# The rows of an image's chunks in DRAM: 64 KB apart, or 72 KB with an unused ninth chunk

## The chip, the core and the metric

The kernel runs on one core of a Trainium2 chip. The core has a matrix engine (TensorE, in profiles PE, its weight loads PEld), three engines for elementwise work (VectorE or DVE, ScalarE or ACT, GpSimd or POOL), and SyncE (SP), which here issues most of the DMA transfers. Sixteen DMA engines move data between the core's own memory (SBUF, 128 partitions) and DRAM. Matrix products land in PSUM, a small memory of its own. The metric is the time of one execution on the device in microseconds (us), the median of several runs.

## The reference, cut to what matters

Sixty-four images of 256 x 256 go through a Fourier neural operator of four layers with 32 channels; its output, joined to 77 rows of text, goes through one transformer layer (attention and a feed-forward part that works on selected rows). All is float32.

```
v = concat(x, gx, gy) @ p_w + p_b                    # 64 images, 32 channels, 256 x 256
for i in range(4):
    x_ft = rfft2(v);  keep 24 x 12 modes;  mix channels with W1, W2;  x1 = irfft2(...)
    x2 = einsum('bcxy,cd->bdxy', v, w_w[i]) + w_b[i]
    v = batch_norm(x1 + x2)                          # mean and variance over all images
    if i < 3: v = relu(v)
h = einsum('bcxy,cu->bxyu', v, q_w) + q_b            # 64 x 256 x 256
h = concat(h, txt);  h = h + attention(layernorm(h));  h = h + ffn(layernorm(h))
```

A field `v` of one image has 32 x 256 x 256 numbers, 8.4 MB. The 64 of them, 537 MB, don't fit into SBUF, so that each layer reads them from DRAM and writes them back.

## The kernel before, in words

**The tensors in DRAM.** `vd` at line 183 is a list of 2 x 64 DRAM tensors, two for each image, that are used in turn: layer 0 writes the first set, layer 1 reads it and writes the second, layer 2 reads the second and writes the first, and the transformer reads the first. Each is `[128, 8, 8, S]` with `S` = 256, float32: 128 rows, one for each SBUF partition; 8 chunks; 8 image rows of 256 numbers in each chunk. A chunk's part of one row is 8 x 256 x 4 B = 8 KB, so that the rows are 8 x 8 KB = 64 KB apart.

**The stages.** `forward_first` reads the input and makes the modes for layer 0 without storing a field. For each layer `mix` then multiplies the modes by their weights and finds the batch norm's factors, and `layer(i, ...)` (line 549) for i = 0, 1, 2 makes the field of all images. After layer 3's `mix` there is no field to be stored: `image_rows` (line 970) reads the stored field of layer 2 directly and projects it to one channel, and `attention`, `select` and `feed_forward` follow.

**A layer.** It goes image by image and chunk by chunk (`b`, `t`). `ld` (line 655, in layers 1 and 2 only) loads one chunk into a tile `vin` with two transfers of 0.5 MB, of four image rows each, issued at line 661. `pre` (line 681) adds up in PSUM the inverse transform (the products at line 687) and, in layers 1 and 2, the channel mixing of the loaded chunk (line 698). `ev` (line 705) evicts the sum through the ReLU into a tile `vo`, half by ScalarE or VectorE at line 710 or 712, as the order says. `st_` (line 716) stores `vo` with two transfers of 0.5 MB, issued at line 719. `turn` (line 721) transposes it; `prod` and `sq` (lines 729 and 741) take the next layer's squares for its batch norm; `y`, `half`, `zt`, `x_`, `xo` and `xs` make the field's modes and store them (lines 750 to 808). `am` loads and scales the mixed modes of a later image (lines 624 to 638), and in layer 0 `lx` loads rows of the input (line 640).

There are four buffers of `vin` in layers 1 and 2 and four of `vo` in all three layers, so that an eviction needs a `vo` tile whose store has landed, and a load needs a `vin` tile that TensorE has read. PSUM is one ring of four tiles, taken in order of release.

**What sets the order.** The layers are written under a manual schedule: `ORDER` (line 128) holds one string of steps for layer 0 and one for layers 1 and 2, and the loop at line 834 runs them in that order for each image, with `@1` for a step of the image after and `@-1` for one of the image before. Every load, store and mode transfer of a layer, apart from the input rows, is issued on SP's queue in this order. In layers 1 and 2 the loads of an image stand among the stores of the image before:

```
"pre5 sqB7@-1 zt1@-1 sqA7@-1 pre6 evA5.a ld2@1 st4 evB5.d st5 turn4 evA6.a prod5 x@-1 "
"evB6.a sqB5 prod6 sqA5 xo@-1 turn5 pre2@1 sqA6 turn6 sqB6 prod4 evA2.a@1 evB2.d@1 "
"sqB4 ld0@1 ld7 sqA4 pre0@1 evB0.d@1 ld3@1 prod2@1 st6 evA0.a@1 turn2@1 sqB2@1 sqA2@1 "
```

**The transformer.** `image_rows` loads a whole chunk `ch` with one transfer of 1 MB (line 990), where each partition's part is 8 KB in one piece, in a pool of seven buffers, and TensorE reads it at line 992. It runs two images ahead.

The instructions that touch `vd` are the store at line 719, the load at line 661 and the load at line 990. All three index a chunk by its number (0 to 7).

Of the kernel before, what the change touches and what calls it, by code (L numbers as in the profile page):

```python
# [9 lines left out]
F32 = mybir.dt.float32  # L10
# [6 lines left out]
S = 256  # L17
# [136 lines left out]
def tile_fno_fusion_transformer(ctx: ExitStack, tc: tile.TileContext, a, cst_d, grid_d, out):  # L154
    nc = tc.nc
    x = a["x"].rearrange("b x y o -> b x (y o)")
    B = x.shape[0]
# [4 lines left out]
    dram = ctx.enter_context(tc.tile_pool(name="dram", bufs=1, space=DRAM))  # L162
# [17 lines left out]
    epsc = const.tile([128, 1], F32, name="epsc")  # L180
    nc.vector.memset(epsc, EPS)

    vd = [dram.tile([128, 8, 8, S], F32, name=f"v{b}_{n}") for n in range(2) for b in range(B)]
    vd = [vd[:B], vd[B:]]
    mix_d = [dram.tile([2, M, 2, B, 32 * C], F32, name=f"mix{i}") for i in range(L)]
    xh_d = [dram.tile([128, B, 144], F32, name=f"xh{i}") for i in range(1, L)]
# [1057 lines left out]
```

## Time and profile before

| What | Value |
|---|---|
| Time, median of 3 runs | 11,274.06 us (11,268.07 to 11,280.38) |
| The profiled execution's own time | 11,266.44 us |
| Its span in the trace | 11,264.7 us |
| Granted TensorE clock, mean | 0.984 |
| Layer 0, first store to last mode store issued | 193 to 2555 us |
| Layer 1, first load to last mode store issued | 2610 to 5562 us |
| Layer 2, likewise | 5620 to 8560 us |
| DMA packets, bytes | 971,776, 3457.30 MB |
| Read from DRAM, written to it | 1733.60 MB, 1696.92 MB |

How to read what follows. The page's first part gives the busy time of each engine with its share of the span; a busy TensorE is not a TensorE at its peak, since its products are pipelined. The row of q1 is SP's DMA queue: packets, MB, and the time its packets took as a share of sixteen engines over the stretch asked for. A row of a transfer has the tile written, the tile read, the queue, how many, KB each, and the median time in us from issue to landing. A row of a stretch has its ends and length in us, the busy us of each engine with the number of instructions, then TensorE's granted clock, the mean busy share of the DMA engines, and GB/s. A row of a wait names the engine and line that waited, what it waited for, us in all, times, and the longest. The chain is the work that ended last, followed back from the end step by step; its shares are of the stretch asked for.

### The profile page before, as it was taken

Reading aid. Unit: us, or ns where it says so; the run is one execution under the profiler, and the core shown is the slowest. Engines: PE = TensorE matmul, PEld = TensorE weight load, DVE = VectorE, ACT = ScalarE, POOL = GpSimd, SP = SyncE. Lnnn points to the kernel's source line nnn. Section 1 sums busy time; section 2 is a strip of 40 time slices with the busy share of each in tenths; the row PEclk is TensorE's granted clock in tenths of the full one; section 3 lists DMA queues with packets and bytes.
Section 4 is the critical chain, followed back from the end, with each engine's and each line's share of the span. In section 5 each row is a group of like instructions: output and inputs, shape, how many; then the busy total and the mean of one; then the engine's idle time right before and its main releaser. Section 6 shows DMA issues by size and latency. Waiting matters only on the chain.

```text
span 11264.7 us, 409247 instructions
## 1 busy us (share of the span) xinstructions
PE 10600.1 (94%) x182550; PEld 5728.7 (51%) x182550; DVE 8446.4 (75%) x10381; ACT 6475.0 (57%) x10673; POOL 1448.0 (13%) x2179
## 2 busy tenths in 40 slices
PE   6999999998999999999799999999996999999999
PEld 3555555554444444444444444444443666666666
DVE  6888888887777777777677777777776666666665
ACT  5777777775656555566556566556664333333333
POOL 1111111110000000000000000000000333333333
PEclk8999999998999999999999999999998999999999
DMA  6776676678999999999899999999998555555553
GB/s 214 248 248 246 246 249 246 246 252 322 381 383 384 378 379 375 376 379 379 316 366 386 379 376 381 382 380 378 375 379 301 224 228 228 225 226 227 225 227 137
DMA packets 971776, 3457.30 MB, mean 307 GB/s; under 512 B 149016, under 2 KB 198552, under 8 KB 903064
## 3 DMA queue, kind: packets, MB, share of 16 engines
q1 hardware_dynamic: 904576, 3366.80, 77.7%
q0 software_dynamic: 58288, 60.60, 2.3%
q8 instruction: 1429, 23.41, 0.8%
q10 hardware_dynamic: 7144, 3.72, 0.1%
q14 instruction: 339, 2.78, 0.1%
HBM read 1733.60 MB, written 1696.92 MB: 305 GB/s over the span
## 4 chain that ended last, share of the span: by engine, by line
PE 61%; DMA 21%; DVE 9%; ACT 4%; issue 3%; SPq 2%; POOL 0%; ACTq 0%; DVEq 0%; POOLq 0%
PE ring L757 15%; DMA v<-vo 11%; PE ring L687 9%; PE ring L735 8%; DMA vin<-v 6%; PE ring L698 5%; PE hp L992 4%; PE ring L667 3%; PE pp L1155 3%; PE pp L1166 3%; PE ring L791 2%; PE pp L1120 2%; DVE vo L712 2%; PE pp L1185 2%; DMA xh<-xo 2%
## 5 line engine op out<-in xcount | busy, mean ns | idle before, releaser
L746 ACT ACTIVATE ring<-ring 128x1024 f32<-128x1024 f32 x3072 | 3115.9, 1014 | 1176.6 <-PE ring L735 1114.9
L724 DVE STREAM_TRANSPOSE t<-vo 128x2048 f32<-128x2048 f32 x1536 | 3465.4, 2286 | 21.1 <-DVE vo L712 0.9
L735 PE MATMUL ring<-vo,w 32*32 32x512 f32 x49152 | 2401.5, 599 | 80.3 <-ACT vo L710 64.2
L712 DVE TENSOR_SCALAR vo<-ring 128x1024 f32<-128x1024 f32 x1280 | 1543.8, 1221 | 1191.4 <-PE ring L698 805.3
L710 ACT ACTIVATE vo<-ring 128x1024 f32<-128x1024 f32 x1792 | 1792.2, 1023 | 1039.9 <-PE ring L698 498.1
L757 PE MATMUL ring<-t,cst 32*32 32x512 f32 x49152 | 2063.5, 599 | 46.4 <-issue 40.2
L757 PEld LDWEIGHTS ring<-t,cst 32*32 32x32 f32 x49152 | 909.6, 103 | 917.1 <-issue 615.9
L735 PEld LDWEIGHTS ring<-vo,w 32*32 32x32 f32 x49152 | 801.3, 103 | 1064.7 <-issue 397.6
L687 PE MATMUL ring<-cst,y 24*128 24x256 f32 x16384 | 1232.6, 403 | 76.8 <-DVE vo L712 59.5
L634 POOL TENSOR_TENSOR ams<-ams,bns 48x512 f32<-48x512 f32 x384 | 401.1, 1045 | 6964.8 <-DMA ams<-mix 6692.2
L698 PE MATMUL ring<-vin,ws 32*32 32x512 f32 x32768 | 1278.0, 603 | 17.9 <-issue 14.0
L687 PEld LDWEIGHTS ring<-cst,y 24*128 24x128 f32 x16384 | 789.8, 185 | 992.8 <-DVE vo L712 389.1
L675 DVE STREAM_TRANSPOSE y<-ring 128x1024 f32<-128x1024 f32 x384 | 762.7, 1986 | 320.0 <-PE ring L667 319.0
L687 PE MATMUL ring<-mv,y 29*128 29x256 f32 x8192 | 705.1, 403 | 36.6 <-ACT ring L746 20.2
L687 PEld LDWEIGHTS ring<-mv,y 29*128 29x128 f32 x8192 | 455.9, 185 | 370.2 <-ACT ring L746 209.8
L791 PEld LDWEIGHTS ring<-cst,zt 128*128 128x128 f32 x4608 | 533.6, 193 | 176.7 <-ACT vo L710 113.8
L767 ACT COPY half<-ring 128x1024 f32<-128x1024 f32 x192 | 194.5, 1013 | 723.9 <-PE ring L757 723.9
L1193 POOL DMA_DIRECT2D out_dram<-o x1024 | 511.2, 508 | 664.8 <-DVE o L1188 622.9
L746 ACT ACTIVATION_READ_ACCUMULATOR ring<-ring 128x1 f32 x3072 | 585.4, 191 | 0.0
L791 PE MATMUL ring<-cst,zt 128*128 128x96 f32 x4608 | 565.6, 280 | 6.2 <-DVE zt L775 6.0
L775 DVE STREAM_TRANSPOSE zt<-ring 128x1024 f32<-128x1024 f32 x192 | 377.4, 1965 | 242.8 <-PE ring L757 242.8
L667 PE MATMUL ring<-ams,cst 49*128 49x512 f32 (+1 forms) x1536 | 450.4, 641 | 108.7 <-POOL ams L634 40.1
(374 smaller groups left out, 9759.8 us busy)
## 6 DMA issues: line engine op xcount, KB each, us to landing
v<-vo SPq DMA_DIRECT2D x3072, 512.0 KB, 7.9
vin<-v SPq DMA_DIRECT2D x2048, 512.0 KB, 9.0
ch<-v SPq DMA_DIRECT2D x512, 1024.0 KB, 13.9
mix<-ob SPq DMA_DIRECT2D x48, 1024.0 KB, 5.3
ams<-mix SPq DMA_DIRECT2D x384, 96.0 KB, 8.0
xin<-in_x_dram SPq DMA_DIRECT2D x16, 1024.0 KB, 8.2
mv<-in_x_dram POOLq DMA_DIRECT2D x256, 64.0 KB, 7.2
out_dram<-o POOLq DMA_DIRECT2D x1024, 16.0 KB, 3.1
```

Of the source, the lines that this page charges most:

```text
L667: nc.tensor.matmul(ps[:, n, :], lhsT=EX[hv, 128 * h:128 * h + 128], rhs=ams[b % 2][hv], start=True, stop=True, skip_group_check=True,)
L675: nc.vector.transpose(y_[b, h].rearrange("p q c -> p c q"), ring[key][0][1].rearrange("p n (c k) -> p (n c) k", k=32),)
L687: nc.tensor.matmul(ps[n][:, 256 * r:256 * r + 256], lhsT=y_[b, t // 4][32 * n:32 * n + K, q:q + 4, :].rearrange("p q c -> p (q c)"), rhs=m ...
L698: nc.tensor.matmul(ps[n][32 * j:32 * j + 32], lhsT=ws[32 * n:32 * n + 32], rhs=v[32 * n:32 * n + 32, 2 * j:2 * j + 2, :], start=False, sto ...
L710: nc.scalar.activation(to, ring[key][h][1], AF.Relu)
L712: nc.vector.tensor_scalar(to, ring[key][h][1], 0.0, None, ALU.max)
L724: nc.vector.transpose(t32[b, t // 2][:, :, 8 * (t % 2):8 * (t % 2) + 8, :].rearrange("p y s c -> p s y c"), vo[b, t].rearrange("p s (y l) ...
L735: nc.tensor.matmul(ps[n][32 * j:32 * j + 32], lhsT=w4[i + 1][32 * n:32 * n + 32], rhs=vo[b, t][32 * n:32 * n + 32, 2 * j:2 * j + 2, :], st ...
L746: nc.scalar.activation(ps, ps, AF.Square, accum_out=acc[:, at:at + 1])
L757: nc.tensor.matmul(ps[n][32 * j:32 * j + 32], lhsT=FYT[32 * n:32 * n + 32, k, :], rhs=t32[b, j][32 * n:32 * n + 32, k].rearrange("p s c -> ...
L791: nc.tensor.matmul(ps[:, 0, 96 * g:96 * g + 96], lhsT=zt_[:, h, k0:k0 + 4, :].rearrange("p k c -> p (k c)"), rhs=FX[:, h, 48 * r:48 * r + ...
L1193: nc.gpsimd.dma_start(out[b, 64 * n + 16 * g:64 * n + 16 * g + 16].rearrange("(p t) d -> p t d", t=2), o[32 * g + 8 * n:32 * g + 8 * n + 8 ...
```

## The change

The DRAM tensors of the fields have nine chunks in place of eight. The loops and the transfers go over chunks 0 to 7 as they did; the ninth is neither written nor read. Rows are 9 x 8 KB = 72 KB apart.

```diff
-    vd = [dram.tile([128, 8, 8, S], F32, name=f"v{b}_{n}") for n in range(2) for b in range(B)]
+    vd = [dram.tile([128, 9, 8, S], F32, name=f"v{b}_{n}") for n in range(2) for b in range(B)]
     vd = [vd[:B], vd[B:]]
```

## The prediction

> **What bounds the kernel now.** I read the page's top, to see how near the engines and the DMA are to full; then stretches of each stage side by side; then the DMA answer for the stages that touch the padded tensors; then waits and chain there.
>
> ```profile
> span 11264.7 us, 409247 instructions
> PE 10600.1 (94%) x182550; PEld 5728.7 (51%) x182550; DVE 8446.4 (75%) x10381; ACT 6475.0 (57%) x10673; POOL 1448.0 (13%) x2179
> q1 hardware_dynamic: 904576, 3366.80, 77.7%
> v<-vo SPq DMA_DIRECT2D x3072, 512.0 KB, 7.9
> vin<-v SPq DMA_DIRECT2D x2048, 512.0 KB, 9.0
> ch<-v SPq DMA_DIRECT2D x512, 1024.0 KB, 13.9
> ```
>
> The three kinds of transfer that the diff touches are 3072 stores and 2048 loads of 0.5 MB and 512 loads of 1 MB: 5120 x 0.524 + 512 x 1.049 = 3221 MB of the 3367 MB on SP's queue. So nearly all of the kernel's DMA traffic changes address, and nothing else changes.
>
> ```profile
> core 0: us, PE busy (x) PEld busy (x) DVE busy (x) ACT busy (x) POOL busy (x), PEclk, DMA share, GB/s
> 1000.00:1500.00 500.00, 485.48 (x9234) 253.98 (x9248) 442.38 (x247) 378.74 (x599) 60.41 (x84) 1.00 0.69 246
> 3000.00:3500.00 500.00, 479.77 (x10350) 227.11 (x10334) 380.21 (x212) 302.51 (x478) 25.10 (x24) 1.00 0.99 382
> 7500.00:8000.00 500.00, 479.57 (x10279) 228.29 (x10277) 376.61 (x211) 301.41 (x477) 23.01 (x22) 1.00 0.99 379
> 9500.00:10500.00 1000.00, 974.77 (x5954) 678.04 (x5953) 673.69 (x2418) 379.70 (x773) 331.50 (x575) 1.00 0.57 225
> ```
>
> These are layer 0 (stores only), layers 1 and 2 (loads and stores), and the transformer (loads only). In layer 0 and in the transformer the DMA engines are busy 69% and 57% of the time while TensorE is busy 97%: there the padded tensors are not the limit. In layers 1 and 2 TensorE has 96%, but the DMA share is 99%. This is where an address can cost or save time. The first and last instruction of each layer put them at 2610 to 5562 us and 5620 to 8560 us, 5892 us together, 46 us an image.
>
> ```profile
> by line: DMA v<-vo 21.0%; PE ring L757 19.0%; DMA vin<-v 12.4%; PE ring L698 10.3%; PE ring L687 9.5%; PE ring L735 7.5%; PE ring L667 4.7%; DVE vo L712 2.8%; issue 2.6%; SPq L661 2.5%; PE ring L791 2.3%; ACT vo L710 2.3%; DMA ams<-mix 1.9%
> ```
>
> ```profile
> ACT vo L710 <- DMA v<-vo: 52.4, 36, 3.3
> DVE vo L712 <- DMA v<-vo: 48.2, 35, 3.3
> PEld ring L698 <- DMA vin<-v: 4.9, 9, 1.1
> ```
>
> Both are of 4000 to 5000 us, in layer 1. About 35% of the chain is DMA (21.0 + 12.4 + 1.9), and the evictions at L710 and L712 wait some 100 us in 1000 for a store to release one of the four `vo` buffers. So a change of the store's or load's speed is felt between two ends: by 35% of it (the chain's share), and by all of it (the DMA share of 0.99).
>
> **The change, part by part.** *Instructions.* None is added, removed or moved. A store at L719 still moves, for each partition, four rows of 256 numbers that lie one after the other: 4 x 256 x 4 B = 4 KB; a load at L990 still 8 KB. So packets stay as many and as large: 0 us. No wait and no queue order changes. *The ninth chunk.* Loops run over eight; 128 x 8 KB = 1 MB an image is never written or read: 0 us. *Addresses.* The 128 rows of one transfer stood 64 KB apart, so that they agreed in the low 16 bits; now they stand 72 KB apart and take eight different positions in a 64 KB frame. This is the only term, and its price is to be read from how long packets take now.
>
> ```profile
> q1 hardware_dynamic: 107162, 374.38, 97.1%
> v<-vo SPq DMA_DIRECT2D x352, 512.0 KB, 9.1
> vin<-v SPq DMA_DIRECT2D x352, 512.0 KB, 9.2
> ```
>
> (The DMA answer for 4000 to 5000 us.) The two kinds make 704 x 128 = 90,112 packets of 4 KB in these 1000 us. The packet records behind this answer give their durations over both layers: 87% take 159 to 161 ns, the mean is 168 ns. 4096 B in 159 ns is 25.8 GB/s, and sixteen engines at that rate make 412 GB/s. Loads and stores both run at this floor, in layer 1 and in layer 2, where the source and the destination tensors change places. In the transformer, 8 KB reads have their own floor of 309 ns (26.5 GB/s) with a mean of 319. A floor that seven packets in eight reach is the DMA engine's own pace, not a memory bank waited for. If rows 64 KB apart fought over the same part of the memory, most packets would be stretched, and the ones of stores and loads differently.
>
> What is left to win is the tail: 168 - 159 = 9 ns a packet. Each 0.5 MB transfer has 8 packets on each of 16 engines; layers 1 and 2 have 2048 stores and 2048 loads. So 1 ns of mean packet time is 4096 x 8 ns = 32.8 us of DMA time, and the whole tail is 9 x 32.8 = 295 us. Is the tail aliasing? I sorted the packets by start into groups of 128. Most groups of either layer have an excess of 0 to 6 ns a packet; the excess sits in three or four groups an image with 20 to 65 ns, at the same place in the order of work (around the loads of chunks 7, 3 and 1, a run of six to eight transfers issued close together where the queue has been worked off and starts anew). (The grouping is rough, by a few us.) In image 0, whose loads are issued in another order, three of the four groups of chunks 3 and 1 have 0 ns. In layer 0, where stores alone use the tensor, the tail too goes by place in the order (54 and 68 ns at the two stores of chunk 3, 6 ns at those of chunks 1 and 2), and by image it is level. A tail that follows the order and not the address is not removed by a new pitch. I take 0 of it, and keep both ends: -295 us if all of it were aliasing and all were felt, and on the other side a new pattern that stretches packets.
>
> For that side the nearest row is layer 0's own packets: mean 176 ns, a 17 ns tail, at a share of 0.69. If the new addresses brought the tail of layers 1 and 2 to that, it would be 8 x 32.8 = 262 us of DMA time, of which 35% to all is felt: +92 to +262 us. In layer 0 and the transformer the same 8 ns is covered by TensorE: the DMA share of 0.69 would go to 0.72. With this cover gone (packets more than 40% longer) those stages would turn DMA-bound as well; nothing here points to that.
>
> **Two rules of the Trainium skill weighed.** The page "DMA: Bandwidth & Descriptors", section "Latency and other measured facts", has a row on HBM row pitch at large powers of two: copies of 128 rows reach 207 GB/s in each direction at a pitch of 512 KiB and 164 at 2 MiB, against 214 with a pad, and it advises a pad of a few KiB. This speaks for a gain. The loss shrinks with the pitch, and the page has no figure for 64 KB; if its smallest loss, 1 - 207/214 = 3.3%, held here, the 168 x 32.8 = 5505 us of packet time would shrink by 180 us at most, an estimate from that page, and the kernel would take some 11,090 us. The packets at their floor here say that the loss is nearer to none. The same page, section "Where 436 GB/s comes from", holds that transfers between HBM and the core are bound by the memory's side, at about 358 GB/s. Were that so, the order of addresses would be what sets the time in layers 1 and 2. The trace has 377 to 382 GB/s in these layers, above that limit, with each engine at a fixed pace; the measurement decides. By the rule the term lies anywhere in -295 to +262; by the row it is 0.
>
> **The sum.** 0 for instructions, 0 for the ninth chunk, 0 for the addresses: the profiled execution of 11,266 us (11,264.7 of span and 2 around it) stays. It lies 8 us under the median of the three runs shown, 11,274, and inside their spread of 11,268 to 11,280. I predict **11,272 us**.
>
> **The rivals.** *Faster, aliasing is real.* For it: the DMA share of 0.99, the tail of 9 ns, the skill's row. Against it: the floor, and the tail's place. Half of the tail gone and felt by half: 295/4 = 74 us, 11,200 us; all of it, 10,980, less what TensorE's 96% takes back: with 4% of idle time in 5892 us it can shorten these layers by 236 us at most, so 11,040. *Slower, the new pitch maps worse.* Rows with equal low bits may be spread evenly by the memory's address map just because they are a power of two apart, and 72 KB may pile several of the sixteen engines on one bank. The place is the same saturated queue of layers 1 and 2, whose late stores hold the `vo` buffers, so L710 and L712 evict later, the ring of PSUM tiles frees later and TensorE's next product starts later. The price is 32.8 us for each ns that is felt; with layer 0's tail and the chain's share of 35% that is +92, or 11,365 us, and with all of it felt 11,535. It decides from 22.5 us, which is 0.7 ns a packet if all is felt and 2 ns at 35%. For it: that point is low, and no run shows this pitch. Against it: no packet kind shows a dependence on address. *The change does nothing at the memory*[...]: that is my forecast.
>
> **How the numbers follow.** A measurement of this kernel tells about 0.2% (22.5 us) from no change. I give the forecast 0.55, faster 0.22, slower 0.23. The sensitivity of 33 us for each ns is why the forecast has no more: a shift of 0.5% in packet time would be seen. The forecast's own range is 11,250 to 11,295. For eight in ten, each rival keeps about one in ten outside: of the gains I cut those over 110 us, of the losses those over 90: 11,160 to 11,360.
>
> **What would show it.** Right: packet floor of 159 ns, mean within 1 ns of 168, 379 to 383 GB/s and a DMA share of 0.98 to 0.99 in the stretches of layers 1 and 2, landings of 9.1 and 9.2 us, 46 us an image, the same chain. Faster: over 390 GB/s there, landings under 9 us, TensorE busy over 97%, and fewer waits of L710 and L712 for stores. Slower: the DMA share stays at 0.99 with under 375 GB/s, landings above 9.5 us, and those waits grow past 100 us in 1000. I would be wrong most simply if the tail is the memory's after all, or if a mapping that looked free at 64 KB is not at 72.

## The result, and the profile after

The changed kernel takes 11,234.72 us in the median of 6 runs (11,230.22 to 11,240.62), the kernel before 11,273.67 us beside it. The ratio is 0.9965, with a 95% interval of 0.9952 to 0.9977: **faster by 0.35%**, some 39 us. The profiled execution after has a span of 11,229.3 us, 35.4 us under the one of before.

The page of the changed kernel, its top and its transfers, in the order shown of before:

```profile
span 11229.3 us, 409247 instructions
PE 10577.1 (94%) x182550; PEld 5734.1 (51%) x182550; DVE 8449.2 (75%) x10381; ACT 6476.7 (58%) x10673; POOL 1447.8 (13%) x2179
q1 hardware_dynamic: 904576, 3366.80, 77.7%
v<-vo SPq DMA_DIRECT2D x3072, 512.0 KB, 7.9
vin<-v SPq DMA_DIRECT2D x2048, 512.0 KB, 9.0
ch<-v SPq DMA_DIRECT2D x512, 1024.0 KB, 12.9
```

Instructions, packets and bytes are the same to the last one, and the share of q1 too: the same transfers in 0.3% less time. Of the transfer rows only the landing of `ch` moved (13.9 to 12.9 us), in the transformer, whose time is as before. Where the time went is seen from where each layer begins and ends (first load or store issued to last mode store issued):

| | before | after | difference |
|---|---|---|---|
| layer 0 | 2346 us | 2343 us | -3 |
| layer 1 | 2952 us | 2930 us | -22 |
| layer 2 | 2941 us | 2929 us | -12 |
| from layer 2's end on | 2715 us | 2715 us | 0 |
| mean 4 KB packet, layers 1 and 2 | 168.2 ns | 167.4 ns | -0.8 |
| mean 4 KB packet, layer 0 | 176.4 ns | 176.6 ns | +0.2 |
| mean 8 KB packet, transformer | 320.6 ns | 320.2 ns | -0.4 |

The lengths are of the trace's own times. The beginnings and ends given with the profile of before lie some 11 us late against the views (there layer 1 runs from 2599 to 5551 us), and layer 0's 193 us should be 209 on that count.

So 34 of the 35 us come from the two layers that load and store, and next to none from the stages that only store or only load. Stretches long enough to smooth the images' beat, of the kernel before:

```profile
core 0: us, PE busy (x) PEld busy (x) DVE busy (x) ACT busy (x) POOL busy (x), PEclk, DMA share, GB/s
1000.00:2400.00 1400.00, 1361.39 (x25865) 713.39 (x25870) 1244.25 (x692) 1064.96 (x1686) 166.92 (x232) 1.00 0.70 247
3000.00:5000.00 2000.00, 1917.85 (x40975) 906.22 (x40961) 1504.11 (x839) 1203.32 (x1896) 94.14 (x90) 1.00 0.98 379
6000.00:8000.00 2000.00, 1917.05 (x41031) 908.99 (x41017) 1506.43 (x842) 1207.77 (x1903) 92.04 (x88) 1.00 0.98 380
9000.00:11000.00 2000.00, 1952.88 (x11922) 1361.23 (x11918) 1349.31 (x4837) 760.62 (x1550) 658.33 (x1145) 1.00 0.58 226
```

and of the changed kernel:

```profile
1000.00:2400.00 1400.00, 1362.60 (x25940) 716.13 (x25936) 1246.46 (x693) 1068.15 (x1692) 167.78 (x233) 1.00 0.70 247
3000.00:5000.00 2000.00, 1924.22 (x41234) 915.67 (x41236) 1515.96 (x845) 1211.46 (x1907) 92.06 (x88) 1.00 0.98 381
6000.00:8000.00 2000.00, 1921.28 (x41184) 917.05 (x41167) 1511.74 (x843) 1215.51 (x1915) 92.03 (x88) 1.00 0.98 381
9000.00:11000.00 2000.00, 1951.51 (x11926) 1358.88 (x11926) 1349.08 (x4844) 760.14 (x1549) 658.55 (x1145) 1.00 0.58 226
```

In layer 1 (the second row of each) the DMA share stays at 0.98 while 381 GB/s move in place of 379, and VectorE gets 845 instructions done in place of 839; layer 2 (the third row) goes from 380 to 381. Layer 0 and the transformer keep 247 and 226 GB/s. TensorE's granted clock is 1.00 in every row, so that it isn't the cause. The waits and the chain of layer 1, 4000 to 5000 us as before:

```profile
ACT vo L710 <- DMA v<-vo: 45.2, 38, 2.6
DVE vo L712 <- DMA v<-vo: 43.8, 37, 2.5
```

```profile
by line: DMA v<-vo 22.7%; PE ring L757 18.9%; DMA vin<-v 13.7%; PE ring L698 9.1%; PE ring L687 8.5%; PE ring L735 7.0%; PE ring L667 4.7%; SPq L661 3.1%; issue 2.6%; ACT vo L710 2.5%; DVE vo L712 2.5%; PE ring L791 2.0%; DMA ams<-mix 1.8%;
```

The evictions wait 89 us for stores where they waited 101 (52.4 + 48.2), and the longest of these waits fell from 3.3 to 2.6 us; the chain is of the same kind.

### The profile page after: what moved, and what is told of

The parts are those of the page before. It is cut to its first block, busy times and chain, and to the rows that moved or that the text cites. A ratio compares the mean times of both kernels' runs of the same rounds, so it can differ in the third digit from the quotient of the medians.

```text
span 11229.3 us, 409247 instructions
## 1 busy us (share of the span) xinstructions
PE 10577.1 (94%) x182550; PEld 5734.1 (51%) x182550; DVE 8449.2 (75%) x10381; ACT 6476.7 (58%) x10673; POOL 1447.8 (13%) x2179
## 4 chain that ended last, share of the span: by engine, by line
PE 63%; DMA 19%; DVE 10%; ACT 3%; issue 3%; SPq 2%; POOL 0%; ACTq 0%; DVEq 0%; POOLq 0%
PE ring L757 16%; DMA v<-vo 10%; PE ring L687 9%; PE ring L735 9%; PE ring L698 6%; DMA vin<-v 5%; PE hp L992 3%; PE ring L667 3%; PE pp L1155 3%; PE pp L1166 3%; PE ring L791 2%; DVE vo L712 2%; PE pp L1120 2%; DMA xh<-xo 2%; PE pp L1185 2%
## 6 DMA issues: line engine op xcount, KB each, us to landing
ch<-v SPq DMA_DIRECT2D x512, 1024.0 KB, 12.9
```

## The experiments

Twelve runs, in three groups; each was compared with the kernel before on the same chip. All but one change only where the fields lie in DRAM. "Layers 1 + 2" is the sum of the two layers in the run's one profile, 5893 us before and 5859 after (5863 when the changed kernel was profiled again). The first diff shows the call as it was and as it is; the others show the new call alone, and the list around it, one tensor for each `n` and `b`, is left out. Distances between images hold if the tensors lie one behind the other; no trace shows an address.

**Which packets are long.** The count that named places in the prediction, and in the first expectation below, is four transfers late. Just before and among the first loads of layer 1, `mix` stores of 1 MB go out on the same queue (from the DMA answer for 2595 to 2632 us of the kernel before):

```profile
vin<-v SPq DMA_DIRECT2D x10, 512.0 KB, 8.7
mix<-ob SPq DMA_DIRECT2D x3, 1024.0 KB
v<-vo SPq DMA_DIRECT2D x2, 512.0 KB
```

Two of them, issued at 2598.5 and 2602.1 us, send 512 packets of 4 KB from the first load on, and a count from that load takes them for the first four loads; by it some packets would start 18 us before their transfer is issued. Without them, the groups of layer 1 that are far over the floor of 159 ns in the kernel before are the second store of chunk 5 (40 ns over), both loads of chunk 0 (46 and 40), both of chunk 3 (27 and 25) and the second store of chunk 6 (24); the other groups have 1 to 10. The order there is st4, st5, ld0, ld7, ld3, st6, ld1: places where it turns from stores to loads or back. Packets carry no name, so that such a count can still mix neighbours.

**1. The images' distance alone.**

```diff
-dram.tile([128, 8, 8, S], F32, name=f"v{b}_{n}")
+dram.tile([144, 8, 8, S], F32, name=f"v{b}_{n}")[0:128]
```

> Rows stay 64 KB apart, but each image's tensor is 9 MB instead of 8 MB, as in the changed kernel (128 rows used of 144). Theory A, the rows of one transfer that agree in their low 16 bits hinder each other: no change, 11,274 us within 15, mean 4 KB packet of layers 1 and 2 at 168.0 ns, the second store of chunk 2 still with about 23 ns over the 159 ns floor. Theory B, what counts is how the tensors of neighbouring images (a load beside a store) stand to each other: 11,235 us, 167.1 ns, that store at 2 to 3 ns over the floor.

Measured: 11,256.35 us, ratio 0.9984 (0.9977 to 0.9991); layers 1 + 2 5877 us, packets 167.5 ns; the store that was watched (the second of chunk 6, by the right count) at 6 to 7 ns over the floor, where it had 22 to 24. Neither theory: by time a gain of under half, by packets nearly the whole (0.7 of 0.8 ns). Where the images stand matters, and by time it isn't all.

**2. A pad of 4 KB.**

```diff
+dram.tile([128, 17, 4, S], F32, name=f"v{b}_{n}")[:, 0:16].rearrange("p (t h) r y -> p t (h r) y", h=2)
```

> Rows 68 KB apart, a pad of 4 KB. Theory A: as good as 72 KB or a little better, since the rows take sixteen positions in a 64 KB frame and not eight: 11,225 to 11,240 us. Theory B: the images stand 8.5 MB apart, so a gain too, 11,235 us. Theory C, the gain is a chance of one placement: anywhere from 11,240 to 11,310 us.

Measured: 11,230.51 us, ratio 0.9967 (0.9955 to 0.9980); layers 1 + 2 5860 us, packets 167.2 ns. The gain of 72 KB again from another distance: not the chance of one placement.

**3. Rows 128 KB apart.**

```diff
+dram.tile([128, 16, 8, S], F32, name=f"v{b}_{n}")
```

> Rows 128 KB apart, eight unused chunks: a larger power of two. Theory A: slower than before, since rows agree in one more address bit: 11,290 to 11,400 us, packets of layers 1 and 2 at 168.5 to 171 ns. Theory B: no change, 11,274 us. Theory C: within 40 us of 11,274 on either side.

Measured: 11,256.13 us, ratio 0.9984 (0.9978 to 0.9991); layers 1 + 2 5881 us, packets 167.7 ns. Theory A expected a loss and found a small gain: agreement in one more low bit does no harm by itself here.

**4. Chunk first.** A chunk fills 1 MB in one piece; a load or store of half of it takes 4 KB in every 8 KB.

```diff
+dram.tile([8, 128, 8, S], F32, name=f"v{b}_{n}").rearrange("t p r y -> p t r y")
```

> Chunk first, then row: [8, 128, 8, 256], so that the rows of one transfer stand 8 KB apart and a load at line 990 is one piece of 1 MB; no byte is unused. Theory A: at least the gain of 72 KB, 11,200 to 11,240 us. Theory B: images stay 8 MB apart and chunks 1 MB, so a load and a store agree in their low 20 bits: no change, 11,274 us.

Measured: 11,376.49 us, ratio 1.0091 (1.0076 to 1.0107): slower, which neither theory expected. Layers 1 + 2 take 6007 us with packets of 172.2 ns. Its stretches of layers 0 and 1 and the transformer:

```profile
1000.00:2400.00 1400.00, 1363.16 (x25876) 713.90 (x25876) 1245.01 (x692) 1065.99 (x1687) 166.67 (x232) 1.00 0.70 247
3000.00:5000.00 2000.00, 1897.87 (x40132) 889.83 (x40116) 1472.38 (x822) 1177.88 (x1858) 91.91 (x88) 1.00 0.98 371
9000.00:11000.00 2000.00, 1951.37 (x11931) 1360.08 (x11930) 1349.89 (x4839) 757.92 (x1547) 658.97 (x1150) 1.00 0.58 225
```

The DMA share is 0.98 as before, but 371 GB/s move in place of 379. Layer 0, which stores to the same compact places, has its 247 GB/s and packets of 176.3 ns; the loads of the transformer, now of 1 MB in one piece, have 225 GB/s and packets of 320.3 ns. The added length is nearly all in the loads, which lie 19.3 ns over the floor in layers 1 and 2 in place of 11.6, while the stores have 7.0 in place of 6.6. A layout that costs 114 us where loads and stores run together costs nothing where either runs alone: TensorE, busy 97% there, would cover some of it, but the packets aren't longer either.

**5. Rows 72 KB apart, images at a power of two.**

```diff
+dram.tile([16 * 128, 8, S], F32, name=f"v{b}_{n}")[0:128 * 9].rearrange("(p t) r y -> p t r y", t=9)
```

> Rows 72 KB apart as in the changed kernel, but each image's tensor is 16 MB, a power of two. Theory A (what counts is how the rows of one transfer stand to each other): the whole gain stays, 11,235 us, packets of layers 1 and 2 at 167.1 ns. Theory B (what counts is how a load and a store that run side by side stand to each other): the images' distance is even again, so the gain falls to that of 128 KB rows or to none, 11,256 to 11,274 us, 167.5 to 168 ns.

Measured: 11,246.42 us, ratio 0.9972 (0.9961 to 0.9984); layers 1 + 2 5874 us, packets 167.4 ns. The ratio can't be told from the changed kernel's, so the rows' distance seems to carry most of the gain without the images'; the layers of its one profile lost 19 us of the 34.

**6. One set of tensors padded.**

```diff
+dram.tile([128, 8 + (n == 0), 8, S], F32, name=f"v{b}_{n}")
```

> Only the first of the two sets of tensors has rows 72 KB apart: layer 0 writes it, layer 1 loads from it and stores to rows 64 KB apart, layer 2 the other way round. Theory A with loads as the ones hindered: layer 1 gains some 17 us, layer 2 nothing. Theory A with stores: the other way round. Theory B: loads and stores no longer move through the memory in step, so both layers gain, as much as the changed kernel or more, 11,225 to 11,240 us.

Measured: 11,260.20 us, ratio 0.9984 (0.9976 to 0.9991): half the gain. Layer 1, which loads from the padded set, takes 2941 us (2952 before), layer 2, which stores to it, 2946 (2941). The times point to loads as the ones helped, but two layers of equal work differ by 11 us in one profile (2952 and 2941 before), and the packets don't agree: the mean fell by 0.6 ns in layer 1 and by 0.5 in layer 2, where the padded stores lost 1.5 ns, about as many as in the changed kernel. It isn't settled. Theory B, by which unequal steps of loads and stores were to be best, falls.

**7. Chunk first, chunks 1 MB + 8 KB apart.**

```diff
+dram.tile([8, 129, 8, S], F32, name=f"v{b}_{n}")[:, 0:128].rearrange("t p r y -> p t r y")
```

> Chunk first, as in the run at 11,376 us, but with chunks 1 MB + 8 KB apart instead of 1 MB; rows stay 8 KB apart, images 8.06 MB. Theory A: rows 8 KB apart are what costs, so it stays slow, 11,340 to 11,390 us. Theory B: different chunks no longer agree in their low 20 bits, so most of the 102 us comes back: 11,235 to 11,290 us.

Measured: 11,345.66 us, ratio 1.0061 (1.0049 to 1.0074); layers 1 + 2 5980 us, packets 171.2 ns. Only about a quarter of the loss came back in the layers (6007 to 5980, against 5893), a third by the median; rows 8 KB apart stay slow.

**8. Rows 512 KB apart.**

```diff
+dram.tile([128, 64, 8, S], F32, name=f"v{b}_{n}")
```

> Rows 512 KB apart, 56 unused chunks. If a power-of-two distance of rows costs what the skill's figures for 512 KiB say (207 against 214 GB/s), packets of layers 1 and 2 take 3.3% longer than in the changed kernel: 172.6 ns, 5.5 x 32.8 = 180 us, 11,415 us. If the distance of rows in one transfer is not what counts (theory B), it stays near 128 KB: 11,240 to 11,280 us.

Measured: 11,346.14 us, ratio 1.0059 (1.0045 to 1.0072); layers 1 + 2 5959 us, packets 169.1 ns. Slower than before, by half of what the Trainium skill's figures made of it (the page "DMA: Bandwidth & Descriptors", "Latency and other measured facts"): against 72 KB its packets are 1.0% longer and its two layers 1.7%, where the page has 3.3%. Layer 0's packets are 175.1 ns and the transformer's 319.3, no longer than before. The page's figures are of copies from DRAM to DRAM, which read and write at once, and that is where this case shows a loss too. The images stand 64 MB apart here, another power of two; no run separates the two distances at this size.

**9. Loads that don't come from DRAM.** The experiment on the tail itself, in layer 1 alone.

```diff
+            if i == 1:
+                fixed = cp.tile([128, 4, S], F32, name="fixed")
+                nc.vector.memset(fixed, 0.25)
...
-                    nc.sync.dma_start(vin[b, t][:, rows], src[b][:, t, rows])
+                    nc.sync.dma_start(vin[b, t][:, rows], fixed if i == 1 else src[b][:, t, rows])
```

> Rows 64 KB apart as before. In layer 1 alone the loads at line 661 take their 0.5 MB from a constant tile in SBUF, so that DRAM is only written there; size, number and order of the transfers stay, and the field that layer 1 reads is a constant, so the numbers from there on are others. Layer 2 is as before and is the yardstick. If the tail of 9 ns over the 159 ns floor comes from loads and stores meeting in DRAM: the packets of layer 1 fall to 160 to 163 ns and layer 1 from 2952 us to 2700 to 2850 us, with layer 2 at 2941. If the tail belongs to the order of work or to SBUF: 167 to 169 ns and 2930 to 2960 us.

Measured: 11,156.06 us, ratio 0.9890 (0.9875 to 0.9905). Layer 1 takes 2828 us, layer 2 2954. (Layer 1 still loads its mixed modes from DRAM, 0.2 MB an image.) Its stretches in layers 1 and 2, and layer 1's DMA answer (4000 to 5000 us):

```profile
3000.00:5000.00 2000.00, 1926.56 (x42656) 923.55 (x42650) 1565.97 (x874) 1253.18 (x1978) 96.19 (x92) 1.00 1.00 395
6000.00:8000.00 2000.00, 1910.43 (x40864) 906.84 (x40832) 1499.21 (x837) 1201.17 (x1894) 92.01 (x88) 1.00 0.98 378
```

```profile
q1 hardware_dynamic: 112075, 391.80, 99.4%
vin<-fixed SPq DMA_DIRECT2D x368, 512.0 KB
v<-vo SPq DMA_DIRECT2D x367, 512.0 KB
```

The same transfers in the same order move 395 GB/s in place of 379, in layer 1 alone, while layer 2 with its loads from DRAM has 378 (380 before). The groups of packets in which the tail sat are gone: the loads of chunks 0 and 3 and the second store of chunk 5, which had 25 to 46 ns over the floor in layer 1 before, have 5; the second store of chunk 6 fell from 24 to 5. The layer's mean packet is 164.4 ns, above the 160 to 163 expected: 5.4 of the 9.2 ns over the floor stay, now spread over nearly all groups (3 to 6 ns each; one has 19). The share of SP's queue rose from 97.1 to 99.4%, so that the gaps between packets shrank as well. Together this is about the layer's 124 us: 3.8 ns less a packet is 3.8 x 16.4 = 62 us, and 2.3% of 2828 us is 65. What went is the price of loads that come from DRAM.

That the price is due to stores beside them is not shown by this run, which takes away the loads' DRAM side and leaves no loads alone. The start of layer 1 in the kernel before speaks for it. There four loads of 0.5 MB and two `mix` stores of 1 MB stand together in the queue, and four of their eight groups of packets lie 41 to 96 ns over the floor. The last four loads before the first field store, chunks 3 and 1 of image 0, have nothing beside them that writes, and are at 14, 0, 1 and 1 ns; in layer 2 likewise, at 3, 2, 3 and 6. With chunk first, too, these loads have 0 to 11. So these loads, alone, run near the floor, in the slowest layout as well. A tail without such meetings exists too: layer 0's stores lie 17 ns over 159, the transformer's loads 11 ns over their 309; but no placement moved those.

**10 to 12. How large the pad must be.** 65 and 100 KB, with the changed kernel beside them.

```diff
+dram.tile([128, 65, S], F32, name=f"v{b}_{n}")[:, 0:64].rearrange("p (t r) y -> p t r y", r=8)
...
+dram.tile([128, 25, 4, S], F32, name=f"v{b}_{n}")[:, 0:16].rearrange("p (t h) r y -> p t (h r) y", h=2)
```

> Rows 65 KB apart, a pad of 1 KB. If any distance that is no power of two spreads the rows: 11,230 to 11,245 us, as with 68 and 72 KB. If a pad must be at least a packet of 4 KB, since the low bits choose little below that: 11,265 to 11,280 us.

Measured: 11,243.92 us, ratio 0.9969 (0.9957 to 0.9980); layers 1 + 2 5878 us, packets 166.9 ns.

> Rows 100 KB apart, 25 times 4 KB. If what counts is that the rows are spread over the low 16 bits in steps of 4 KB: the same as 68 KB, 11,225 to 11,240 us. If more distance helps by itself: under 11,220 us.

Measured: 11,238.40 us, ratio 0.9967 (0.9954 to 0.9979); layers 1 + 2 5860 us, packets 167.0 ns.

> The changed kernel beside 65 and 100 KB on one chip, for the comparison of the pads: 11,235 us, ratio 0.9965.

Measured: 11,246.18 us, ratio 0.9971 (0.9959 to 0.9982); layers 1 + 2 5863 us, packets 167.5 ns. By the ratio the four pads of 1, 4, 8 and 36 KB can't be told apart (65 KB's one profile has only 15 us off the layers); 1 KB is enough, and no placement that was tried beats the changed kernel by more than the measurement can tell.

## Why the prediction was right or wrong

The time came out at 11,235 us, inside the range of 11,160 to 11,360, but not at the likeliest case of no change (11,272 us, its own range from 11,250): what happened is the first rival, given 0.22, at about half of its 74 us. The range held because it left room for both rivals; the forecast's own reason for it did not hold. Most of its signs of being right came true all the same (167.4 ns, 381 GB/s, a share of 0.98, landings of 8.9 and 9.3 us, the same chain): they were too coarse for 35 us, and of the signs of a gain only the fewer waits for stores and the stores' landing under 9 us showed.

*What bounds the kernel: held.* All movement of all twelve runs is in layers 1 and 2. Layer 0 stays within 2343 to 2350 us and what follows layer 2 within 2711 to 2715, from the best placement to the worst.

*Instructions and the ninth chunk at 0: held.* The counts are equal.

*A floor reached by most packets means that no memory is waited for: half held.* The floor stayed at 159 ns in every run, with loads from SBUF too, which fits the DMA engines' own pace. But a floor that 87% of packets reach says nothing on the other 13%, and they were worth 295 us by the prediction's own count.

*"A tail that follows the order and not the address is not removed by a new pitch. I take 0 of it": this is the step that failed.* The term measured 0.8 ns of the 9, and 34 us in the two layers. The tail does follow the order of work, but the order also says which loads stand beside which stores; with the loads taken from SBUF (experiment 9) the hot groups vanished with the order untouched. That layer 0's tail goes by order too was no help: it is another tail, which no placement moved by more than 1.5 ns (175.1 to 176.9 ns). To call one cause after looking at two stages was the mistake. That image 0 had loads at the floor was read as a matter of their order; by the right count, too, its loads of chunks 3 and 1 are at 0 to 14 ns, and what sets them apart is that no store runs beside them. What the new pitch takes of the tail sits at the tail's own places, and mostly in the stores: over layers 1 and 2 the stores' packets fell from 6.6 to 5.1 ns over the floor, the loads' stayed (11.6 and 11.5). In layer 1 the second store of chunk 6 went from 24 to 2 ns and the second load of chunk 0 from 40 to 25, while the first load of chunk 3 rose from 27 to 45.

*The sensitivity of 32.8 us for each ns: right in size, not complete.* 0.8 x 32.8 = 27 us, and the two layers lost 34. For chunk first it gives 4.0 x 32.8 = 131 against 114 measured, for 512 KB 0.9 x 32.8 = 30 against 66. The packets' durations are not the whole; in experiment 9 the gaps between packets were as large a term. The felt part lies near the upper end (all of it, by the DMA share), not at the chain's 35%.

*The rule on power-of-two pitches* gave 180 us at most and spoke for a gain: its sign was right at 64 KB, its size five times too large, and whether for its reason stays open. *The rule of 358 GB/s* is no limit here (381, and 395 with the loads from SBUF): the section takes it as half of what two cores share, and here one core runs. Its point, that the memory's side has a say in these layers, was right.

*The slower rival* found nothing at 72 KB. That a placement can cost was right, however: 8 KB and 512 KB between rows cost 67 to 102 us in the median.

*Small slips in its numbers*, which carry no term: 11,266 us lies just under the spread of 11,268 to 11,280, not inside it, and the mean 8 KB packet is 320.6 ns over the whole transformer, not 319.

*What stays open.* Which property of an address does it. Theory A (rows of one transfer that agree in low bits) foretold the gain at 68 KB, agrees with those at 65 and 100 KB and with the direction at 512, and failed at 128 KB and at 8 KB. Theory B (load and store in step) failed in runs 5, 6 and 7, but alone says why the images' distance matters in run 1. What is shown is that loads from DRAM cost layer 1 124 us against loads from SBUF, and that the placement of rows and images changes the time of the two layers that load and store, and of no other stage by more than 4 us. That it is loads and stores meeting in DRAM that slow each other fits all of this and the start of the layers, but no run sent the stores elsewhere. The gain was mostly in the stores' packets and the losses in the loads', which no theory here explains, and no run shows how addresses map to the memory.

## What to carry to other kernels

Where a stage reads and writes DRAM at once with the DMA engines near their full share, a small pad on the rows' distance is a cheap thing to try: 1 KB did as much as 36 KB here, and it costs no instruction. It gave nothing in the stages that only load or only store. And don't take the most compact layout for the safe one: 4 KB pieces that stand 8 KB apart in one block of 1 MB were the slowest tried. When packets mostly run at their floor, count what the others are worth, and test their cause in the stage itself by taking one side of the traffic away. Before packets are sorted into places by counting, look what else goes through the queue.

## What was not expected of the hardware

With each chunk packed into one block of 1 MB, loads and stores together moved 371 GB/s in place of 379, at a cost of 0.9% of the whole time, though stores alone (247 GB/s) and loads alone (225 in place of 226) were as before. And a layer that loads from DRAM and stores to it took 4% longer than one with its loads from SBUF (2952 and 2828 us), at the same number and size of transfers.
